# Pairwise attention scores with the sender term negated: minima in place of maxima, and the sign carried by the matmul's weights

## The chip, the cores and the metric

The kernel runs on one core of a Trainium2 chip. A core has four engines that this document speaks of: PE (TensorE, matrix multiply, fed by a weight load that the profile lists as PEld), DVE (VectorE, elementwise), ACT (ScalarE, activation functions) and POOL (GpSimd, elementwise). PE and the other engines meet through semaphores; PE writes to PSUM, the accumulator memory, and the rest lives in SBUF. The metric is the device time of one execution in microseconds (us), lower is better. Before the change it is 5019.07 us, the median of three runs that lie between 5017.83 and 5020.0 us.

## The reference

Input x holds 64 graphs of 256 nodes with 128 features; `adj` is one 256x256 matrix that all graphs share. Four layers follow one another, each of them x = x + layer(relu(layernorm(x))). Layers 1 to 3 are a sigmoid-gated aggregation, an attention with tanh and exp, and a gated recurrent unit with five steps. They are not touched by the change. Layer 0 is the costly one, and the change is all in it:

```python
s1 = jnp.einsum('bkf,ef->bke', x, W1)      # W = adj: W1 = adj[:, :128], W2 = adj[:, 128:]
s2 = jnp.einsum('bkf,ef->bke', x, W2)      # 256 features e
pre = s1[:, :, None, :] + s2[:, None, :, :] + b_lin
h = jnp.where(pre >= 0, pre, 0.2 * pre)
e = jnp.einsum('bije,e->bij', h, a) + bias
attn = jax.nn.softmax(e, axis=2)
out = jax.nn.sigmoid(jnp.einsum('bij,bjf->bif', attn, x))
```

For each graph, every ordered pair (i, j) of its 256 x 256 node pairs has 256 features that go through a leaky relu and are summed with the weights `a`. That is over a thousand million relus in all, and they are computed one by one.

## The kernel before, in words

**What is computed for a pair.** The leaky relu is split into a linear part and 0.8 times a relu. Of the linear part, what depends on i alone cancels in the softmax over j, and what depends on j comes from two matmuls (`v2_rep`, line 732). The features are reordered and scaled by |a| when the weights `w_p` are prepared (lines 219 to 304), so that a feature's weight is only +0.8 or -0.8; 256 features make two halves `ec` of 128, one feature on each partition. The relu tile of a node i is 128 features x 256 senders j, and there are 256 nodes x 2 halves of these for each of 64 graphs.

**Two ways to write a tile.** ACT computes relu(s2 + s1), with s1 as a bias that is one number per partition (line 698). DVE and POOL compute max(s2, -s1) instead, from a tile `s1n` that holds -s1 (DVE line 680, POOL line 703). The two differ by s1, which doesn't depend on j and so cancels in the softmax. `s2` is a copy in SBUF, DVE reads it in PSUM (`s2_ps`), and ACT after its first two half batches in a PSUM copy of its own (`s2_act`).

**Batches.** A batch is a tile `r` of eight node tiles (4 groups `g` of 32 nodes, times 2 places `k`), in a pool of 12 buffers (`BUFS`). It is made in two halves (`g2`), and either half can be made by DVE, ACT or POOL; DVE can make both at once. PE multiplies a batch by a window of `a_win` (lines 764 to 767): the window is 32 columns wide, zero but for one column with +-0.8, so the sum over 128 features lands in one row of the scores `e_ps`. Four matmuls with 32 columns each, one for each g, go side by side in the four column groups of PE. Each fp32 matmul shows as two instructions in the profile. A batch of `ec` 0 takes one matmul of 512 columns for each g, both k in one; a batch of `ec` 1 has different weights for its two k, and takes two matmuls of 256 columns for each g.

**Merges.** Two node rows take four batches: for each row one with `ec` 0 and one with `ec` 1. When at least `SPARE` = 5 finished batches wait for PE, two rows are made as three batches instead (`begin`, lines 609 to 623): in the first two, DVE adds max(s2, -s1) of the second feature half onto the places k = 0 of the `ec` 0 batch (`merge`, line 722), four instructions a batch; the third batch (`two`) holds the second feature half of the nodes k = 1 of both rows. So a merged pair of rows costs PE one batch less, and DVE eight merge instructions in place of eight tiles made by anyone.

**The order is planned when the program is built.** `Model` (lines 38 to 52) keeps a clock for each engine, and the last loop of the kernel gives the next piece of work to the engine whose clock allows it first. Its prices are constants: 365 ns for an ACT tile, 454 for a POOL tile, 1131 and 2198 ns for a half and a whole batch on DVE, 392 for a merge, 858 for a batch on PE. Other work (the layers of earlier graphs, the preparation of later ones) comes from generators, the chains, whose steps are fitted in between; helpers `act`, `dve`, `mm` add each step's price. Each engine then runs its instructions in the planned order, whatever their real durations are.

**Preparation of a group.** Groups are one or two graphs (`GROUPS`: 34 groups, 30 of them with two). For the first, `first_head` (line 475) computes s1 and s2; for the 33 others `head` (line 506) does the layer norm, the transposition and s1, and `senders` (line 555) s2. Here ACT writes `s1` (line 523) and `s1n` (line 525) from the same PSUM tile, each twice a group: 66 instructions each, 60 of them 512 wide. In `first_head` DVE writes `s1n` (line 492) and ACT `s1` (line 500).

Of the kernel before, what the change touches and what calls it, by code (L numbers as in the profile page):

```python
# [12 lines left out]
P = 128  # L13
# [42 lines left out]
def kernel(ctx: ExitStack, tc: tile.TileContext, ins: dict, out: bass.AP):  # L56
# [102 lines left out]
    make_identity(nc, ident)  # L159
    neg_half = constant([P, 4], "neg_half")  # L160
    nc.gpsimd.memset(neg_half, -0.5)
    a_win = constant([P, 2, 63], "a_win")
    nc.vector.memset(a_win, 0.0)
    a_rep = lent([P, 2, P], "a_rep", "h_t")
    nc.vector.memset(a_rep, 0.2)
# [46 lines left out]
    v2_rep = constant([P, P], "v2_rep")  # L212
    w_p = constant([P, 2, N], "w_p")
    blin_p = constant([P, 2], "blin_p")
    blin_n = constant([P, 2], "blin_n")
    left2 = constant([P, P], "left2")
    left_b = constant([P, 1], "left_b")

    def constants0():
# [56 lines left out]
                )  # L276
        yield "dve"
        dve(2).tensor_copy(blin_p, b_ps)
        dve(2).tensor_scalar(blin_n, b_ps, -1.0, None, ALU.mult)
        for half in (1, 0):  # L280
            yield "act"
            act(N).copy(w_p[:, half, :], p[:, half, :])
        counts["w_p"] += 2
        yield "dve"
        for c in range(2):
# [13 lines left out]
        dve(P).tensor_copy(v2_rep, v2_ps)  # L299

        for c in range(2):
            w = a_win[:, c, 31:32]
            dve(1).tensor_scalar(w, p_two[:, c : c + 1], n_pos, None, ALU.is_lt)
            dve(1).tensor_scalar(w, w, 1.6, -0.8, ALU.mult, ALU.add)

# [167 lines left out]
    def first_head(xt, to, snd):  # L475

        G, _, W = sizes(xt)
        h = yield from ln_relu(ap, xt, "h0", "h0", at=LANDS)
        h_t = yield from transpose_blocks(ap, h, "h0t", psum_h)
        to.update(h=h, h_t=h_t)  # L480
        yield "pe", lambda: counts["w_p"] > 1
        s2_ps, s1_ps = psum_h([P, 2, N], "s2_ps"), psum_a([P, 2, W], "s1_ps")
        for half, p in ((1, s2_ps), (0, s1_ps)):
            for ec in range(2):
                mm(
                    p[:, ec, :], lhsT=w_p[:, half, bass.ts(ec, P)], rhs=flat(h_t),
                    start=True, stop=True,
                )
        yield "dve"
        s1n = ap.tile([P, 2, W], F32, tag="s1n", name="s1n")  # L490
        for ec in range(2):
            dve(W, 1).tensor_scalar(
                s1n[:, ec, :], s1_ps[:, ec, :], -1.0, blin_n[:, ec : ec + 1], ALU.mult, ALU.add
            )
        yield "act"
        s2 = ap.tile([P, 2, N], F32, tag="s2", name="s2")
        act(2 * N).copy(s2, s2_ps)
        s1 = ap.tile([P, 2, W], F32, tag="s1", name="s1")
        for ec in range(2):
            act(W, 1, more=27).activation(  # L500
                s1[:, ec, :], s1_ps[:, ec, :], AF.Identity, bias=blin_p[:, ec : ec + 1]
            )
        to.update(s1=s1, s1n=s1n)
        snd.update(s2=s2, s2_ps=s2_ps)

    def head(xt, to):
        G, _, W = sizes(xt)
        h = yield from ln_relu(ap, xt, "h0", "h0")
        h_t = yield from transpose_blocks(ap, h, "h0t", psum_h, settled)
        to.update(h=h, h_t=h_t)  # L510
        if counts["left"] > 0:
            yield from bounds(to)
        for ec in range(2):
            yield "pe", lambda: counts["w_p"] > 0
            p = psum_h([P, W], "s1_ps")
            mm(
                p, lhsT=w_p[:, 0, bass.ts(ec, P)], rhs=flat(h_t), start=True, stop=True
            )
            yield "act", lambda: counts["w_p"] > 1
            if ec == 0:  # L520
                s1 = ap.tile([P, 2, W], F32, tag="s1", name="s1")
                s1n = ap.tile([P, 2, W], F32, tag="s1n", name="s1n")
            act(W, 1, more=27).activation(s1[:, ec, :], p, AF.Identity, bias=blin_p[:, ec : ec + 1])
            yield "act"
            act(W, 1, more=27).activation(
                s1n[:, ec, :], p, AF.Identity, bias=blin_n[:, ec : ec + 1], scale=-1.0
            )
        to.update(s1=s1, s1n=s1n)

    def bounds(of):  # L530

# [48 lines left out]
    class Pairs:  # L580
# [5 lines left out]
        def __init__(self, g, b, of, snd):  # L586
            self.g, self.b, self.of, self.snd = g, b, of, snd
            self.row = 0
            self.todo = []
            self.merges = []  # L590
            self.batches = []
            self.opened = False
            self.owned, self.by_act = {}, 0

            self.s1n_v = of["s1n"][:, :, bass.ts(b, N)].rearrange(
                "p c (k g t) -> p c g k t", k=2, g=4
            )
            self.s1n_b = of["s1n"][:, :, bass.ts(b, N)].rearrange(
                "p c (k g t) -> p c k g t", k=2, g=4
            )  # L600

# [7 lines left out]
        def begin(self):  # L609
            waiting = sum(x["halves"] == 2 for x in self.batches)  # L610
            merged = waiting >= SPARE and self.row < 31
            t = self.row

            if merged:
                kinds = ((t, 0, True, False), (t + 1, 0, True, False), (t, 1, False, True))
            else:
                kinds = ((t, 0, False, False), (t, 1, False, False))
            for t, ec, on_top, two in kinds:
                batch = {
                    "t": t, "ec": ec, "merged": on_top, "two": two, "halves": 0, "ready": 0.0  # L620
                }
                self.todo += [(batch, ec, 0), (batch, ec, 1)]
            self.row += 2 if merged else 1
# [35 lines left out]
        def make(self, who):  # L659
# [6 lines left out]
                self.batches.append(batch)  # L666
            r, t = batch["r"], batch["t"]
            s2 = self.snd["s2"] if who == "pool" else self.own(who)
            s1, s1n = self.of["s1"], self.of["s1n"]
            if who == "dve":  # L670
                whole = g2 == 0 and self.todo and self.todo[0][0] is batch
                if whole:
                    self.todo.pop(0)
                n = 4 if whole else 2
                if batch["two"]:
                    s1n = self.s1n_b[:, ec, 1, 2 * g2 : 2 * g2 + n, t : t + 2].unsqueeze(3)
                else:
                    s1n = self.s1n_v[:, ec, 2 * g2 : 2 * g2 + n, :, t : t + 1]
                model.op("dve", model.WHOLE if whole else model.HALF)
                nc.vector.tensor_tensor(  # L680
                    r[:, 2 * g2 : 2 * g2 + n, :, :],
                    s2[:, ec : ec + 1, :].unsqueeze(1).to_broadcast([P, n, 2, N]),
                    s1n.to_broadcast([P, n, 2, N]),
                    ALU.max,
                )
                if whole:
                    if batch["merged"]:
                        self.merges.append((model.t[who] + LAG[who], batch, 0))
                        g2 = 1
                    else:  # L690
                        self.whole(batch, who)
            else:
                for g, ic, i in self.nodes(batch, g2):
                    if g > 2 * g2 or ic:
                        yield
                    if who == "act":
                        model.op("act", model.TILE["act"] + 42 * (s2 is self.snd["s2"]))
                        nc.scalar.activation(  # L698
                            r[:, g, ic, :], s2[:, ec, :], AF.Relu, bias=s1[:, ec, i : i + 1]
                        )  # L700
                    else:
                        model.op("pool", model.TILE["pool"])
                        nc.gpsimd.tensor_scalar(  # L703
                            r[:, g, ic, :], s2[:, ec, :], FLT_MAX, s1n[:, ec, i : i + 1],
                            ALU.min, ALU.max,
                        )
            if batch["merged"]:
                self.merges.append((model.t[who] + LAG[who], batch, g2))
# [3 lines left out]
        def merge(self):  # L712

            _, batch, g2 = self.merges.pop(0)
            r = batch["r"]
            for g, ic, i in self.nodes(batch, g2):
                if ic:
                    continue
                if g > 2 * g2:
                    yield  # L720
                model.op("dve", model.MERGE)
                nc.vector.scalar_tensor_tensor(  # L722
                    r[:, g, ic, :], self.own("dve")[:, 1, :], self.of["s1n"][:, 1, i : i + 1],
                    r[:, g, ic, :], ALU.max, ALU.add,
                )
            self.whole(batch, "dve")

# [15 lines left out]
        def multiply(self):  # L743
# [10 lines left out]
                parts = ((1, t, 1, 0), (1, t + 1, 1, 1))  # L754
            elif batch["ec"]:
                parts = ((0, t, 0, 0), (1, t, 1, 1))
            else:
                parts = ((slice(0, 2), t, 0, slice(0, 2)),)
            for ic, t, sign, k in parts:
                for g in range(4):  # L760
                    to, of = self.e_ps[bass.ts(g, 32), ic, :], r[:, g, k, :]
                    if len(parts) == 1:
                        to, of = to.rearrange("p a b -> p (a b)"), flat(of)
                    nc.tensor.matmul(  # L764
                        to, lhsT=a_win[:, sign, 31 - t : 63 - t], rhs=of,
                        start=False, stop=self.over, skip_group_check=True,
                    )

# [543 lines left out]
```

## Time and profile before

| what | value |
|---|---|
| three runs, median (range) | 5019.07 us (5017.83 to 5020.0) |
| the profiled execution: span from first to last instruction | 5017.8 us |
| busy share PE / DVE / ACT / POOL | 99% / 98% / 98% / 95% |
| weight loads (PEld) | 46% |
| DMA, mean of the span | 6 GB/s |
| mean granted TensorE clock | 0.999 |

The profiled execution's own time is its span, 5017.8 us, some 1.3 us under the median of the runs. The page lists groups of instructions by line, engine and operation, with the names of the tiles that are written and read, the number of instructions, the busy time of the group in us, the mean duration of one in ns, and then the engine's idle time before them and what ended it. Instructions of ACT, DVE and PE overlap their neighbours at the ends: the mean duration of an ACT tile, 871 ns, is the time through the pipeline, and the distance from one start to the next is what a further instruction costs. The timeline gives such starts. The chain of waits follows the work that ended last back from the end, so a piece's duration there is the time it held up what came after it.

### The profile page before, as it was taken

The numbers are of one execution on the slowest core, as the hardware profiler recorded it, in microseconds if no ns is written. First come the engines' busy times: TensorE is split into PE (matmuls) and PEld (weight loads), VectorE is DVE, ScalarE is ACT, GpSimd is POOL, SyncE is SP. The second block draws the span as 40 slices with busy tenths as digits, with TensorE's granted clock in tenths as the row PEclk, the third lists the DMA queues.
The fourth block names the chain that finished last, engine by engine and source line by source line (L and its number), as shares of the span: only waits on it lengthen the run. The fifth ranks groups of instructions, "written<-read, shape, count | busy, mean of one in ns | idle before, by whom it ended". The sixth has DMA issues, their size and how long they took to land.

```text
span 5017.8 us, 176085 instructions
## 1 busy us (share of the span) xinstructions
PE 4985.7 (99%) x69627; PEld 2291.3 (46%) x69627; DVE 4895.7 (98%) x8591; ACT 4922.9 (98%) x12912; POOL 4778.0 (95%) x10637
## 2 busy tenths in 40 slices
PE   9999999999999999999999999999999999999998
PEld 4444444444444444444444444444444444444444
DVE  9999999999999999999999999999999999999994
ACT  8999999999999999999999999999999999999994
POOL 8999999999999999999999999999999999999881
PEclk9999999999999999999999999999999999999999
DMA  0000000000000000000000000000000000000000
GB/s 22 4 6 2 5 6 7 6 2 6 7 6 7 2 6 6 7 6 2 6 8 4 7 4 6 6 7 4 4 6 6 7 7 2 5 5 4 4 4 8
DMA packets 56109, 29.56 MB, mean 6 GB/s; under 512 B 20336, under 2 KB 55280, under 8 KB 55280
## 3 DMA queue, kind: packets, MB, share of 16 engines
q1 hardware_dynamic: 54736, 18.04, 1.5%
q8 instruction: 546, 8.95, 0.7%
q14 instruction: 283, 2.32, 0.2%
q10 hardware_dynamic: 544, 0.26, 0.0%
HBM read 9.84 MB, written 8.45 MB: 4 GB/s over the span
## 4 chain that ended last, share of the span: by engine, by line
PE 92%; DVE 4%; ACT 3%; issue 1%; POOL 0%; DMA 0%; DVEq 0%; ACTq 0%; POOLq 0%
PE e_ps L764 56%; PE gate_ps L109 8%; PE hv_ps L109 6%; PE m_ps L109 5%; PE s_ps L109 3%; DVE r L680 3%; PE o_ps L109 2%; PE e_ps L109 2%; ACT r L698 2%; PE rc_ps L109 2%; PE hn_ps L116 1%; PE rsum_ps L109 1%; PE e_ps L116 1%; PE h_t_ps L116 1%; DVE r L722 1%
## 5 line engine op out<-in xcount | busy, mean ns | idle before, releaser
L703 POOL TENSOR_SCALAR r<-s,s1n 128x256 f32<-128x256 f32 x10012 | 4528.5, 476 | 79.4 <-PE e_ps L764 36.4
L698 ACT ACTIVATE r<-s_act,s 128x256 f32<-128x256 f32 x9664 | 4170.7, 871 | 7.6 <-PE e_ps L764 6.0
L764 PE MATMUL e_ps<-r,a_win 128*32 128x256 f32 (+1 forms) x40144 | 3258.1, 467 | 3.4 <-DVE r L680 3.3
L680 DVE TENSOR_TENSOR r<-s_ps,s1n 128x1024 f32<-128x1024 f32 (+1 forms) x1281 | 2291.0, 1824 | 3.9 <-PE e_ps L764 3.9
L764 PEld LDWEIGHTS e_ps<-r,a_win 128*32 128x32 f32 x40144 | 1279.9, 110 | 1574.3 <-issue 853.6
L722 DVE SCALAR_TENSOR_TENSOR r<-s_ps,s1n,r 128x256 f32<-128x256 f32 x4504 | 1852.6, 471 | 1.7 <-POOL r L703 1.0
L698 ACT ACTIVATE r<-s,s 128x256 f32<-128x256 f32 x512 | 298.2, 1006 | 0.1
L109 PE MATMUL m_ps<-adj_t,hn 128*32 128x256 f32 x4096 | 248.0, 381 | 1.6 <-ACT hn L1089 1.6
L455 ACT ACTIVATE h<-x,bsh,brs 128x128 f32<-128x128 f32 x384 | 229.6, 850 | 5.6 <-POOL bsh L449 4.7
L109 PEld LDWEIGHTS m_ps<-adj_t,hn 128*32 128x32 f32 x4096 | 133.0, 110 | 118.2 <-issue 32.2
L1066 ACT ACTIVATE gate_ps<-gate_ps,bz 128x512 f32<-128x512 f32 (+1 forms) x170 | 170.8, 1005 | 2.7 <-PE gate_ps L109 2.7
L1068 ACT ACTIVATE hv_ps<-hv_ps,bh 128x512 f32<-128x512 f32 (+1 forms) x170 | 166.4, 979 | 6.5 <-PE hv_ps L109 6.5
L1038 ACT COPY m_t<-m_ps 128x512 f32<-128x512 f32 (+1 forms) x170 | 161.4, 949 | 9.3 <-PE m_ps L109 9.3
L1048 ACT ACTIVATE m_ps<-gate_ps,br 128x512 f32<-128x512 f32 (+1 forms) x170 | 161.0, 949 | 8.9 <-PE gate_ps L109 7.2
L109 PE MATMUL hv_ps<-rh,u_th 128*32 128x512 f32 (+1 forms) x1360 | 168.4, 567 | 0.9 <-DVE rh L1051 0.9
L109 PE MATMUL gate_ps<-m_t,t_w_w 128*32 128x512 f32 (+1 forms) x1360 | 168.1, 568 | 0.3 <-ACT m_t L1038 0.2
L109 PE MATMUL hv_ps<-m_t,t_w_w 128*32 128x512 f32 (+1 forms) x1360 | 168.5, 567 | 0.0
L109 PE MATMUL gate_ps<-m_t,w_t 128*32 128x512 f32 (+1 forms) x1360 | 168.4, 568 | 0.0
L1089 ACT COPY hn<-hn_ps 128x512 f32<-128x512 f32 (+1 forms) x136 | 126.5, 930 | 18.2 <-PE hn_ps L116 18.0
L109 PE MATMUL gate_ps<-hf,u_t 128*32 128x512 f32 (+1 forms) x1088 | 135.4, 567 | 0.0
L109 PE MATMUL s_ps<-h0t,w_p 128*32 128x256 f32 (+1 forms) x1568 | 134.9, 445 | 0.5 <-ACT h0t L471 0.5
L447 POOL TENSOR_TENSOR brs<-bve,neg_half 128x4 f32<-128x4 f32 (+1 forms) x136 | 133.5, 982 | 0.0
(213 smaller groups left out, 4388.1 us busy)
## 6 DMA issues: line engine op xcount, KB each, us to landing
xt<-in_x_dram SPq DMA_DIRECT2D x30, 256.0 KB
out_dram<-y SPq DMA_DIRECT2D x30, 256.0 KB
row<-rows SPq DMA_DIRECT2D x128, 0.5 KB
xt<-in_x_dram SPq DMA_DIRECT2D x4, 128.0 KB
out_dram<-y SPq DMA_DIRECT2D x4, 128.0 KB
bound<-row SPq DMA_DIRECT2D x30, 2.0 KB
raw_L_gnn_w_w<-in_L_gnn_w_w_dram SPq DMA_DIRECT2D x3, 128.0 KB
adj_n<-in_adj_dram ACTq DMA_DIRECT2D x1, 256.0 KB
```

The costliest lines, as they stand in the source:

```text
L109: nc.tensor.matmul(out[bass.ts(c, 32), :], lhsT=lhsT[:, bass.ts(c, 32)], rhs=rhs, **flags)
L116: nc.tensor.transpose(out, src, ident)
L455: act(P, 2, 1).activation(h[:, g, :], xt[:, g, :], AF.Relu, bias=shift[:, g : g + 1], scale=rstd[:, g : g + 1],)
L680: nc.vector.tensor_tensor(r[:, 2 * g2 : 2 * g2 + n, :, :], s2[:, ec : ec + 1, :].unsqueeze(1).to_broadcast([P, n, 2, N]), s1n.to_broadcast ...
L698: nc.scalar.activation(r[:, g, ic, :], s2[:, ec, :], AF.Relu, bias=s1[:, ec, i : i + 1])
L703: nc.gpsimd.tensor_scalar(r[:, g, ic, :], s2[:, ec, :], FLT_MAX, s1n[:, ec, i : i + 1], ALU.min, ALU.max,)
L722: nc.vector.scalar_tensor_tensor(r[:, g, ic, :], self.own("dve")[:, 1, :], self.of["s1n"][:, 1, i : i + 1], r[:, g, ic, :], ALU.max, ALU.add,)
L764: nc.tensor.matmul(to, lhsT=a_win[:, sign, 31 - t : 63 - t], rhs=of, start=False, stop=self.over, skip_group_check=True,)
L1038: act(W).copy(m_t, m_ps)
L1048: act(W, 1).activation(t_r, g_ps, AF.Tanh, bias=br, scale=0.5)
L1066: act(W, 1).activation(t_z, g_ps, AF.Tanh, bias=bz, scale=0.5)
L1068: act(W, 1).activation(cand, hv_ps, AF.Tanh, bias=bh)
```

## The change

`w_p`'s second half gets a factor -1, so s2 comes out negated (s2n). DVE and POOL then compute min(s2n, s1), which is -max(s2, -s1), and ACT computes relu(-s2n + s1) as before by giving its instruction the scale -1. So a half batch made by ACT is positive, one made by DVE or POOL negative. `a_win` gets a second copy with the opposite sign, and each half batch carries a mark (`up`, 1 for ACT) that selects the copy. The tile `s1n` is no longer made, nor is `blin_n`; in `first_head` DVE now writes `s1`, and ACT's two instructions there go. A merge keeps the place k = 0 negative: it subtracts an ACT half from the minimum, and adds any other. In a merged `ec` 0 batch with at least one ACT half, k = 0 is then negative and k = 1 positive, so its matmul of 512 columns for each g becomes two of 256 columns with their own weights. The planner's constants and its price of a batch stay as they are.

```diff
-    a_win = constant([P, 2, 63], "a_win")
+    a_win = constant([P, 2, 2, 63], "a_win")
...
-        dve(2).tensor_scalar(blin_n, b_ps, -1.0, None, ALU.mult)
         for half in (1, 0):
             yield "act"
-            act(N).copy(w_p[:, half, :], p[:, half, :])
+            act(N).activation(
+                w_p[:, half, :], p[:, half, :], AF.Copy, scale=-1.0 if half else 1.0
+            )
...
-            w = a_win[:, c, 31:32]
+            w, w_n = (a_win[:, up, c, 31:32] for up in (1, 0))
             dve(1).tensor_scalar(w, p_two[:, c : c + 1], n_pos, None, ALU.is_lt)
             dve(1).tensor_scalar(w, w, 1.6, -0.8, ALU.mult, ALU.add)
+            dve(1).tensor_scalar(w_n, w, -1.0, None, ALU.mult)
@@ -487,20 +488,15 @@
             dve(W, 1).tensor_scalar(
-                s1n[:, ec, :], s1_ps[:, ec, :], -1.0, blin_n[:, ec : ec + 1], ALU.mult, ALU.add
+                s1[:, ec, :], s1_ps[:, ec, :], blin_p[:, ec : ec + 1], None, ALU.add
             )
...
-        s1 = ap.tile([P, 2, W], F32, tag="s1", name="s1")
-        for ec in range(2):
-            act(W, 1, more=27).activation(
-                s1[:, ec, :], s1_ps[:, ec, :], AF.Identity, bias=blin_p[:, ec : ec + 1]
-            )
@@ -519,13 +515,8 @@
             act(W, 1, more=27).activation(s1[:, ec, :], p, AF.Identity, bias=blin_p[:, ec : ec + 1])
-            yield "act"
-            act(W, 1, more=27).activation(
-                s1n[:, ec, :], p, AF.Identity, bias=blin_n[:, ec : ec + 1], scale=-1.0
-            )
@@ -666,22 +658,22 @@
                 nc.vector.tensor_tensor(
                     r[:, 2 * g2 : 2 * g2 + n, :, :],
                     s2[:, ec : ec + 1, :].unsqueeze(1).to_broadcast([P, n, 2, N]),
-                    s1n.to_broadcast([P, n, 2, N]),
-                    ALU.max,
+                    s1.to_broadcast([P, n, 2, N]),
+                    ALU.min,
                 )
...
+                batch["up"][g2] = int(who == "act")
...
                         nc.scalar.activation(
-                            r[:, g, ic, :], s2[:, ec, :], AF.Relu, bias=s1[:, ec, i : i + 1]
+                            r[:, g, ic, :], s2[:, ec, :], AF.Relu, bias=s1[:, ec, i : i + 1],
+                            scale=-1.0,
                         )
...
                         nc.gpsimd.tensor_scalar(
-                            r[:, g, ic, :], s2[:, ec, :], FLT_MAX, s1n[:, ec, i : i + 1],
-                            ALU.min, ALU.max,
+                            r[:, g, ic, :], s2[:, ec, :], FLT_MAX, s1[:, ec, i : i + 1],
+                            ALU.min, ALU.min,
                         )
@@ -720,8 +714,8 @@
                 nc.vector.scalar_tensor_tensor(
-                    r[:, g, ic, :], self.own("dve")[:, 1, :], self.of["s1n"][:, 1, i : i + 1],
-                    r[:, g, ic, :], ALU.max, ALU.add,
+                    r[:, g, ic, :], self.own("dve")[:, 1, :], self.of["s1"][:, 1, i : i + 1],
+                    r[:, g, ic, :], ALU.min, ALU.subtract if up else ALU.add,
                 )
@@ -754,15 +748,18 @@
             elif batch["ec"]:
                 parts = ((0, t, 0, 0), (1, t, 1, 1))
+            elif batch["merged"] and any(batch["up"]):
+                parts = ((0, t, 0, 0), (1, t, 0, 1))
             else:
                 parts = ((slice(0, 2), t, 0, slice(0, 2)),)
             for ic, t, sign, k in parts:
                 for g in range(4):
                     to, of = self.e_ps[bass.ts(g, 32), ic, :], r[:, g, k, :]
+                    up = 0 if batch["merged"] and k == 0 else batch["up"][g // 2]
                     if len(parts) == 1:
                         to, of = to.rearrange("p a b -> p (a b)"), flat(of)
                     nc.tensor.matmul(
-                        to, lhsT=a_win[:, sign, 31 - t : 63 - t], rhs=of,
+                        to, lhsT=a_win[:, up, sign, 31 - t : 63 - t], rhs=of,
                         start=False, stop=self.over, skip_group_check=True,
                     )
```

## The prediction

> **What bounds the kernel now.** I read the page's busy times first; they leave the question open, because all four engines are nearly full. The table by stretches, taken over the body of the run without its first 60 and last 138 us, sharpens it, and PE's waits in the same stretch decide it (who waited for whom: us, times, longest).
>
> ```profile
> PE 4985.7 (99%) x69627; PEld 2291.3 (46%) x69627; DVE 4895.7 (98%) x8591; ACT 4922.9 (98%) x12912; POOL 4778.0 (95%) x10637
> ```
> ```profile
> 60.00:4880.00 4820.00, 4816.00 (x67235) 2211.84 (x67236) 4777.39 (x8355) 4803.91 (x12615) 4699.93 (x10448) 1.00 0.02 5
> ```
> ```profile
> PE left_ps L109 <- DVE r L680: 1.2, 2, 0.8
> PE e_ps L764 <- DVE r L680: 1.1, 2, 0.8
> ```
>
> In 4820 us PE stands idle for 4, and its longest visible wait is 0.8 us. Idle in the same order are DVE 43, ACT 16 and POOL 120 us. So PE binds at every moment, and the makers of tiles (DVE, ACT, POOL) are within a few per cent of it: the planner has traded PE's batches against DVE's merges until both are full. The time falls only if PE gets fewer or cheaper batches. The groups that carry layer 0, and pieces of the chain of waits (start, us held, what):
>
> ```profile
> L703 POOL TENSOR_SCALAR r<-s,s1n 128x256 f32<-128x256 f32 x10012 | 4528.5, 476 | 79.4 <-PE e_ps L764 36.4 <-DVE v_rep L299 9.5 <-issue 7.6
> L698 ACT ACTIVATE r<-s_act,s 128x256 f32<-128x256 f32 x9664 | 4170.7, 871 | 7.6 <-PE e_ps L764 6.0 <-POOL bmm L445 1.2
> L764 PE MATMUL e_ps<-r,a_win 128*32 128x512 f32 x16384 | 2038.8, 593 | 2.6 <-DVE r L680 2.6
> L722 DVE SCALAR_TENSOR_TENSOR r<-s_ps,s1n,r 128x256 f32<-128x256 f32 x4504 | 1852.6, 471 | 1.7 <-POOL r L703 1.0 <-ACT r L698 0.5
> L764 PE MATMUL e_ps<-r,a_win 128*32 128x256 f32 x23760 | 1527.9, 380 | 0.8 <-DVE r L680 0.7
> ...
> L698 ACT ACTIVATE r<-s,s 128x256 f32<-128x256 f32 x512 | 298.2, 1006 | 0.1
> ```
> ```profile
> 2499.61 0.86 PE e_ps L764 x8
> 2500.46 0.86 PE e_ps L109 x16
> ...
> 2518.71 0.87 PE e_ps L109 x32
> ...
> 2520.44 1.72 PE hv_ps L109 x16
> ...
> 2538.40 1.73 PE m_ps L109 x32
> ```
>
> Counting: 4504 merges at eight a pair are 563 merged pairs of rows. 64 graphs x 32 rows are 2048 rows; two batches each, less one a merged pair, are 3533 batches. The matmuls agree: 2048 batches of `ec` 0 with 8 instructions of 512 columns are 16384, and 2048 - 563 = 1485 others with 16 of 256 are 23760. A batch holds PE for 0.86 us in either form.
>
> **What the change removes.** ACT's 66 instructions of line 525. Their price is the distance between starts, not their span:
>
> ```profile
> 1976.24 1.09 ACT L523 ACTIVATE s<-s_ps,blin_p 128x512 f32<-128x512 f32 x1
> 1976.81 0.88 ACT L698 ACTIVATE r<-s_act,s 128x256 f32<-128x256 f32 x1
> 1977.17 1.11 ACT L525 ACTIVATE s1n<-s_ps,blin_n 128x512 f32<-128x512 f32 x1
> 1977.74 1.27 ACT L698 ACTIVATE r<-s_act,s 128x256 f32<-128x256 f32 x2
> ```
>
> A 512-wide one takes 0.57 us, a 256-wide tile 0.36: 60 x 0.57 + 6 x 0.36 = 36 us of ACT. The planner prices 0.578 and 0.365, so 36.9, and 0.7 for the two instructions of `first_head`: 37.6 us. Nobody on PE's path waits for them, so their own removal gives PE nothing; it pays through the planner. 37.6 us are 103 ACT tiles. The makers' rate is 1/0.365 + 1/0.454 + 8/2.198 = 8.58 tiles a us. One more merged pair saves PE 0.858 us, saves the makers 8 tiles and costs DVE 8 x 0.392 = 3.14 us, which is 11.4 of its tiles: net 3.4 tiles. If the plan shortens by d us, it has d/0.858 pairs more, and the makers lose 8.58 d tiles: 103 = 8.58 d + 3.4 d/0.858, so d = 8.2 us, with 9.6 more pairs. The ends: 0, if ACT's freed time only turns into waiting for buffers (POOL's row shows 36.4 us of waits for PE to free one); and 30 pairs or 26 us, if the makers lose nothing by a shorter run because their true idle time (16 to 120 us above) covers it. I take 8, because the planner sees its own prices and both sides full, and keep 0 and 26 for the range.
>
> **What it adds on PE.** Merged `ec` 0 batches with an ACT half go from 8 instructions of 512 columns to 16 of 256. There are 2 x 563 = 1126 merged ones. ACT makes 9664 + 512 of 28264 tiles, 36%; a batch has two halves, so 36% to 59% of them contain one of ACT, 405 to 665: I take 535. By the chain, 32 instructions of 256 hold PE for 1.73 us and 16 of 512 for 1.72, so a split costs 5 ns (0 to 10 by the rounding): 535 x 5 = 3 us, ends 0 and 11 us if all 1126 cost 10. The 128-column piece, 0.87 us for four times as many instructions, shows the same: no visible fixed part. The planner does not price this, and PE has no idle time to cover it, so all of it is added. Twice the weight loads lie under matmuls, as they already do in the 1485 batches of 256 columns; PEld is busy 46%.
>
> The Trainium skill, "TensorEngine Tiling (Array Packing)", section Instruction Overhead, speaks against the split: each matmul has an overhead of about 60 cycles. At the 2.4 GHz of its page "Trainium Kernel Development and Optimization" (section NeuronCore Architecture) that is an estimated 25 ns for each of two more rounds of four matmuls, so 535 x 50 ns = 27 us and a run of 5038 us. The rows above say 5 ns a batch, and I go by them.
>
> **What it moves, at no cost.** DVE's max becomes min, and its add sometimes subtract: among 128x512 tensor_tensors a subtract (line 1072) has a mean of 677 ns, a multiplication (line 974) 678; 1 in 678 of DVE's 4144 us on lines 680 and 722 is 6 us either way, under its 43 idle. ACT's scale -1: line 525 has it, line 523 has not, and both step by 0.57 us, so 0; the reading leaves 10 ns either way, 102 us over ACT's 10176 tiles, against a cover of 16 us idle, so this end is kept with the POOL rival below. POOL's second operation max becomes min, and no row of before shows that pair. The nearest row is line 703 itself, same form and width; the lowest end is the same operation on 4 columns (0.19 us, against 0.45 a tile: 0.26 less), the highest a power on 4 columns, 0.83 us more than the 0.19:
>
> ```profile
> 2401.30 18.98 POOL L703 TENSOR_SCALAR r<-s,s1n 128x256 f32<-128x256 f32 x42
> 2420.37 0.19 POOL L444 TENSOR_SCALAR bve<-bmv 128x4 f32<-128x4 f32 x1
> ...
> 2420.80 1.02 POOL L447 TENSOR_TENSOR brs<-bve,neg_half 128x4 f32<-128x4 f32 x1
> ```
>
> Both ends are far off; I take 0. A cheaper POOL tile would gain little, because the order is fixed and PE is the bound. At the start, `first_head` loses two ACT instructions (0.84 us) but DVE gets two more tiny ones for `a_win` (0.15 each) ahead of its first batch: within half a us, taken as 0. No wait is added: readers of `s1` wait for ACT as those of `s1n` did, and no DMA or queue is touched.
>
> **The new order** is a term of its own. PE's chain has pieces of 0.99 where 0.86 would do, and weight loads wait for a maker some 650 times in the body (389 for POOL, 125 for ACT, 95 and 45 for DVE); at 0.13 us each that is an estimated 85 us, and a tenth more or less is 8 us. In the last 118 us PE is idle 18; a third of that, 6, may move. I take 0 for both, and 8 to 10 us as the spread around each case.
>
> **Sum.** 5017.8 - 8.2 + 2.7 = 5012.3 for the span; with the 1.3 us by which the median stands above it, 5014 us.
>
> **The rivals.**
> - *The gain goes nowhere* (ACT idles or waits for buffers, merges stay near 4504): 5019 + 3 = 5022 us. For it: POOL's and ACT's waits for PE's buffers. Against: the planner merges whenever five batches wait, so any surplus turns into merges.
> - *More merges than the balance*: 26 us less, 3 more, 4996 us. For it: idle time of DVE and POOL; against: the planner doesn't see that idle time.
> - *POOL's min with min is slower than min with max*, the one that ends on the slower side. Place: line 703, 9867 tiles in the body. The planner would go on giving POOL as many tiles. It decides from 120 us / 9867 = 12 ns a tile (3%) on; beyond that each ns costs 9.9 us, so at 25 ns 5014 + 128 = 5142 us. For it: POOL's operations do differ (power 1.02 against 0.19). Against: the same form, one comparison for another.
> - *The split costs more than 5 ns*, by weight loads that no longer hide: at two uncovered loads of 110 ns a batch, 535 x 0.22 = 118 us, 5129. Against: the 1485 batches that are split already hold PE 0.86 us.
>
> The Trainium skill, "GPSIMD Engine Reference", section 3.1, says that loops of at most two operations an element are bound by ports at 1.03 cycles an element; that would make all pairs equal, at an estimated 0.22 us for 256 columns at 1.2 GHz. The trace has 0.45, so that bound is not what sets this tile, and the page can't close the POOL rival.
>
> **How the numbers follow.** A measurement tells 0.2%, 10 us, from no change: faster is under 5009, slower over 5029. Likeliest 0.62, with its own range 5004 to 5024 (about a fifth under 5009); gain nowhere 0.18; more merges 0.12; slow POOL (or ACT) 0.05; dear split 0.03. Faster: 0.62 x 0.22 + 0.12 = 0.26; slower: 0.08 and some 0.02 of the tails, 0.10; the rest, 0.64, within 0.2%. The range for 8 in 10 leaves out the two dear cases and about half of the many-merges case: 4998 to 5030.
>
> **What would show it.** Right: line 525 gone, line 523 still 66; merges (line 722) up from 4504 to about 4580, ACT tiles up by some 80, POOL's down by some 20; the 512-column group of line 764 down by 8 for each split batch, about 4300, the 256-column group up by about 8400; PE still without waits. The split is dear if the sixteens of line 764 hold over 0.87 us each in the chain; the POOL rival shows as a step over 0.46 us. Wrong would make me, above all, a plan whose merges go down, or a tail laid out differently.

## The result and the profile after

The changed kernel takes 11592.83 us, the median of six runs, against 5019.97 us for the kernel before beside it: 2.309 times as long, with a 95% interval from 2.307 to 2.312. I had forecast 5014 us within 4998 to 5030. The term that failed is POOL's, which I had put at 0.

The page of the changed kernel: span, busy times, granted clock by slices, the shares of the chain that ended last, and the groups of layer 0 (line 697 is POOL's tile, 761 PE's batch, 716 the merge, 691 ACT's tile).

```profile
span 11591.5 us, 188542 instructions
...
PE 7343.1 (63%) x75947; PEld 2890.9 (25%) x75947; DVE 5056.6 (44%) x8674; ACT 5020.1 (43%) x12924; POOL 11435.9 (99%) x10629
...
PEclk9988787788887878878877777878878888778878
...
POOL 56%; issue 11%; PE 4%; DVE 1%; ACT 0%; POOLq 0%; DVEq 0%; ACTq 0%
...
L697 POOL TENSOR_SCALAR r<-s,s 128x256 f32<-128x256 f32 x10004 | 11184.5, 1139 | 30.2 <-DVE s L493 9.1
L761 PE MATMUL e_ps<-r,a_win 128*32 128x256 f32 (+1 forms) x46464 | 5331.8, 496 | 2482.6 <-POOL r L697 2366.0
L716 DVE SCALAR_TENSOR_TENSOR r<-s_ps,s,r 128x256 f32<-128x256 f32 x4600 | 2016.3, 479 | 4665.4 <-POOL r L697 4553.8
L691 ACT ACTIVATE r<-s_act,s 128x256 f32<-128x256 f32 x9744 | 3797.7, 538 | 466.1 <-PE e_ps L761 444.8
```

Before, four engines were full. Now POOL is full, PE is 63% busy and DVE and ACT under 45%. POOL's group has 10004 tiles where it had 10012, but a mean of 1139 ns where it had 476. Most of the others' idle time goes back to POOL: DVE's merges waited 4554 us for POOL's tiles and PE's batches 2366. The timeline of POOL gives the distance from start to start (start, us, engine, what, count):

```profile
2499.11 17.89 POOL L697 TENSOR_SCALAR r<-s,s 128x256 f32<-128x256 f32 x16
2517.08 0.20 POOL L445 TENSOR_SCALAR bve<-bmv 128x4 f32<-128x4 f32 x1
```

16 tiles in 17.89 us are 1.12 us a tile, against 0.45 before (42 in 18.98; the medians of the distances are 1.117 and 0.451). The difference times 10004 is 6.7 ms more on POOL, and the run is 6.57 ms longer. POOL's small multiply-add on 4 columns costs what it cost before.

### The profile page after: what moved, and what is told of

Same layout as the page of the kernel before. It is cut to its first block, busy times and chain, and to the rows that moved or that the text cites. A ratio compares the mean times of both kernels' runs of the same rounds, so it can differ in the third digit from the quotient of the medians.

```text
span 11591.5 us, 188542 instructions
## 1 busy us (share of the span) xinstructions
PE 7343.1 (63%) x75947; PEld 2890.9 (25%) x75947; DVE 5056.6 (44%) x8674; ACT 5020.1 (43%) x12924; POOL 11435.9 (99%) x10629
## 4 chain that ended last, share of the span: by engine, by line
POOL 56%; issue 11%; PE 4%; DVE 1%; ACT 0%; POOLq 0%; DVEq 0%; ACTq 0%
POOL r L697 55%; PE e_ps L761 2%; POOL brs L448 1%; PE gate_ps L109 1%; DVE r L672 0%; PE hv_ps L109 0%; PE m_ps L109 0%; DVE r L716 0%; ACT r L691 0%; POOL x1b L883 0%; POOL bsh L450 0%; POOL bmm L446 0%; POOL bve L445 0%; PE s_ps L109 0%; PE o_ps L109 0%
## 5 line engine op out<-in xcount | busy, mean ns | idle before, releaser
L697 POOL TENSOR_SCALAR r<-s,s 128x256 f32<-128x256 f32 x10004 | 11184.5, 1139 | 30.2 <-DVE s L493 9.1
L761 PE MATMUL e_ps<-r,a_win 128*32 128x256 f32 (+1 forms) x46464 | 5331.8, 496 | 2482.6 <-POOL r L697 2366.0
L716 DVE SCALAR_TENSOR_TENSOR r<-s_ps,s,r 128x256 f32<-128x256 f32 x4600 | 2016.3, 479 | 4665.4 <-POOL r L697 4553.8
L691 ACT ACTIVATE r<-s_act,s 128x256 f32<-128x256 f32 x9744 | 3797.7, 538 | 466.1 <-PE e_ps L761 444.8
L761 PEld LDWEIGHTS e_ps<-r,a_win 128*32 128x32 f32 x46464 | 1760.4, 122 | 5575.1 <-POOL r L697 4005.5
L672 DVE TENSOR_TENSOR r<-s_ps,s 128x2048 f32<-128x2048 f32 (+1 forms) x1267 | 2252.6, 1813 | 124.9 <-PE e_ps L761 122.7
L109 PE MATMUL m_ps<-adj_t,hn 128*32 128x256 f32 x4096 | 325.0, 405 | 2.7 <-ACT hn L1086 2.5
L109 PE MATMUL gate_ps<-m_t,w_t 128*32 128x512 f32 (+1 forms) x1360 | 264.8, 679 | 0.0
L116 PE MATMUL h_t_ps<-ident,h 128*128 128x128 f32 x256 | 82.8, 393 | 275.3 <-ACT h L456 274.1
L116 PE MATMUL hn_ps<-ident,hf 128*128 128x128 f32 x512 | 104.8, 335 | 142.2 <-DVE hf L1075 139.5
```

The source lines that it names most:

```text
L109: nc.tensor.matmul(out[bass.ts(c, 32), :], lhsT=lhsT[:, bass.ts(c, 32)], rhs=rhs, **flags)
L116: nc.tensor.transpose(out, src, ident)
L672: nc.vector.tensor_tensor(r[:, 2 * g2 : 2 * g2 + n, :, :], s2[:, ec : ec + 1, :].unsqueeze(1).to_broadcast([P, n, 2, N]), s1.to_broadcast( ...
L691: nc.scalar.activation(r[:, g, ic, :], s2[:, ec, :], AF.Relu, bias=s1[:, ec, i : i + 1], scale=-1.0,)
L697: nc.gpsimd.tensor_scalar(r[:, g, ic, :], s2[:, ec, :], FLT_MAX, s1[:, ec, i : i + 1], ALU.min, ALU.min,)
L716: nc.vector.scalar_tensor_tensor(r[:, g, ic, :], self.own("dve")[:, 1, :], self.of["s1"][:, 1, i : i + 1], r[:, g, ic, :], ALU.min, ALU.su ...
```

## The experiments

Two theories could explain a slow POOL. **A**: the pair of operations min with min is itself slow there. **B**: the pair is not to blame, but something around it is (the operand `s1`, its buffer, the sharing of SBUF with the other engines). Each ratio below compares a run with runs of the kernel before on the same chip.

**The pairs by themselves.** A small kernel that leaves out the computation and has 24 POOL instructions for each pair. In the trace they take turns in twos: one min with max, one min with min, and so on. For example:

```diff
+    for _ in range(24):
+        nc.gpsimd.tensor_scalar(min_max[:, 0:256], s[:, 0:256], FLT_MAX, c[:, 0:1], ALU.min, ALU.max)
+    for _ in range(24):
+        nc.gpsimd.tensor_scalar(min_min[:, 0:256], s[:, 0:256], FLT_MAX, c[:, 0:1], ALU.min, ALU.min)
```

> A small kernel that leaves out the whole computation and writes zeros: 12 or 24 POOL instructions in a row for each pair of operations, on 128x256 fp32 from one SBUF tile, three pairs also on DVE, and two pairs in four widths. Theory A (the pair itself is slow on POOL): min with max 0.45 us from start to start, min with min about 1.12 us; the slow pair's extra should grow with the width if it is per element. Theory B (the pair is not the cause; something around it in the changed kernel slows POOL: the operand s1, its buffer, or sharing SBUF with DVE): both pairs 0.45 us here. Both theories: DVE's pairs do not differ. Open for both: whether max with min, or a single min, is at the fast price.

The groups of that kernel, a line for each pair; the name of the tile says the pair, `ptr` that the first scalar is the pointer and the second the constant, `only` a single operation (count, then busy us and mean ns):

```profile
L95 POOL TENSOR_SCALAR min_min_wide<-s,c 128x1024 f32<-128x1024 f32 x12 | 44.3, 3694 | 0.0
L35 POOL TENSOR_SCALAR min_min<-s,c 128x256 f32<-128x256 f32 x24 | 27.7, 1155 | 0.0
L50 POOL TENSOR_SCALAR mult_min<-s,c 128x256 f32<-128x256 f32 x24 | 27.4, 1144 | 0.1
...
L41 POOL TENSOR_SCALAR max_max<-s,c 128x256 f32<-128x256 f32 x24 | 27.3, 1139 | 0.0
...
L47 POOL TENSOR_SCALAR add_max<-s,c 128x256 f32<-128x256 f32 x24 | 27.3, 1137 | 0.0
...
L38 POOL TENSOR_SCALAR max_min<-s,c 128x256 f32<-128x256 f32 x24 | 27.2, 1133 | 0.0
...
L62 POOL TENSOR_SCALAR only_min<-s,c 128x256 f32<-128x256 f32 x24 | 22.1, 923 | 0.0
L86 POOL TENSOR_SCALAR min_max_wide<-s,c 128x1024 f32<-128x1024 f32 x12 | 13.4, 1114 | 0.0
L32 POOL TENSOR_SCALAR min_max<-s,c 128x256 f32<-128x256 f32 x24 | 11.6, 482 | 4.4 <-DMA c<-in_adj_dram 4.4
L56 POOL TENSOR_SCALAR mult_add<-s,c 128x256 f32<-128x256 f32 x24 | 11.5, 478 | 2.2
L68 POOL TENSOR_SCALAR ptr_min_max<-s,c 128x256 f32<-128x256 f32 x24 | 11.4, 474 | 0.0
...
L89 POOL TENSOR_SCALAR min_min_four<-s,c 128x4 f32<-128x4 f32 x12 | 3.7, 309 | 0.0
L80 POOL TENSOR_SCALAR min_max_four<-s,c 128x4 f32<-128x4 f32 x12 | 3.2, 268 | 0.0
```

Theory A holds, in a sharper form than I had it. Of the 14 two-operation variants tried (11 pairs, three of them also with their scalars exchanged), min with max and mult with add last 474 to 482 ns, min with max in both orders of its scalars. All the others last 1133 to 1155, max with min among them, and a single operation 923, almost twice a fast pair. For mult with add this holds of the duration alone: it ran in turn with min with add, and some 0.09 us of idle time stood between the two, so that from its start to the next one's 0.57 us passed, where min with max took 0.45. Why is open.

```profile
205.22 0.48 POOL L56 TENSOR_SCALAR mult_add<-s,c 128x256 f32<-128x256 f32 x1
205.79 1.15 POOL L59 TENSOR_SCALAR min_add<-s,c 128x256 f32<-128x256 f32 x1
```

From 256 to 1024 columns min with max grows by (1114 - 482) / 768 = 0.82 ns a column, min with min by (3694 - 1155) / 768 = 3.3. On 4 columns they are only 41 ns apart. On DVE I had expected no difference; the three pairs tried have means of 410 to 508 ns, min with min between the others, so none is slow as on POOL.

The Trainium skill, "GPSIMD Engine Reference", section 3.1, gives 1.03 cycles an element for loops of at most two operations, an estimated 0.86 ns at the 1.2 GHz of "Trainium Kernel Development and Optimization" (section NeuronCore Architecture). The slope of min with max, 0.82, agrees with it; that of min with min, also two operations, is four times as steep, so the number of operations does not tell the price.

**The pair exchanged in the kernel before, and a second slow pair in the changed one.**

```diff
-                            r[:, g, ic, :], s2[:, ec, :], FLT_MAX, s1n[:, ec, i : i + 1],
-                            ALU.min, ALU.max,
+                            r[:, g, ic, :], s2[:, ec, :], -FLT_MAX, s1n[:, ec, i : i + 1],
+                            ALU.max, ALU.max,
```

> The kernel before with one edit: POOL computes max(s2, -FLT_MAX) and then the max with s1n, in place of min with FLT_MAX and then max; same values, same planned order. Theory A, if two equal operations are slow: 10012 tiles at 1.12 us on POOL, so some 11400 to 11700 us. Theory B: 5020 us, no change.

11574 us, one run, with the old operands, the old order and everything else of the kernel before. Theory B is out: the pair alone makes a loss of 6555 us (11574.3 - 5019.4), where the changed kernel lost 6573. Its group by shape:

```profile
L703 POOL TENSOR_SCALAR r<-s,s1n 128x256 f32<-128x256 f32 x10012 | 11168.8, 1135 | 27.6 <-DVE v_rep L299 9.8 <-PE e_ps L764 4.1 <-issue 0.2
```

```diff
-                            r[:, g, ic, :], s2[:, ec, :], FLT_MAX, s1[:, ec, i : i + 1],
-                            ALU.min, ALU.min,
+                            r[:, g, ic, :], s2[:, ec, :], -FLT_MAX, s1[:, ec, i : i + 1],
+                            ALU.max, ALU.min,
```

> The changed kernel with one edit: POOL computes max(s2n, -FLT_MAX) and then the min with s1, in place of min with FLT_MAX and then min; same values. Theory A, if max with min is a fast pair as min with max is: POOL tiles back at 0.45 us, and the rest of the prediction holds, about 5014 us (5004 to 5024). Theory A, if any pair but min with max is slow: about 11600 us. Theory B: about 11600 us, since operands and buffers stay as in the changed kernel.

11568.1 us (ratio 2.305, 2.302 to 2.308): max with min is as slow, as it is in the small kernel. My guess that its mirror image shares the fast price was wrong.

**The change with a fast pair.** The same value can be had as a min with `s1` and then a max with -FLT_MAX, which changes nothing:

```diff
-                            r[:, g, ic, :], s2[:, ec, :], FLT_MAX, s1[:, ec, i : i + 1],
-                            ALU.min, ALU.min,
+                            r[:, g, ic, :], s2[:, ec, :], s1[:, ec, i : i + 1], -FLT_MAX,
+                            ALU.min, ALU.max,
```

> The changed kernel with POOL's two operations the other way about: first the min with s1, then a max with -FLT_MAX, so the pair is min with max; same values, same planned order. Theory A (the pair, and nothing else, made the kernel slow): POOL tiles at 0.45 us and the other terms of the prediction as they stand, with the 814 split batches counted in the changed kernel at the 3 ns each that splitting alone has measured (3.0 us for 1126): 5017.8 - 8.2 + 2.4 and 1.3, 5013 us (5004 to 5024). Theory B, that something else in the change slows POOL or the rest: far above 5030 us.

5017.07 us, against 5021.94 for the kernel before: ratio 0.9990, 0.9982 to 0.9999. So the rest of the change is worth 4.9 us, a tenth of a per cent, and the interval only just excludes zero gain. It is the fastest version of this study. Its page, and the groups by shape:

```profile
span 5012.7 us, 188542 instructions
...
PE 4978.0 (99%) x75947; PEld 2494.4 (50%) x75947; DVE 4890.7 (98%) x8674; ACT 4915.8 (98%) x12924; POOL 4742.0 (95%) x10629
```
```profile
L697 POOL TENSOR_SCALAR r<-s,s 128x256 f32<-128x256 f32 x10004 | 4492.8, 477 | 92.9 <-PE e_ps L761 51.7 <-DVE s L493 9.7 <-ACT r L691 4.7
...
L761 PE MATMUL e_ps<-r,a_win 128*32 128x256 f32 x36592 | 2240.0, 380 | 3.8 <-DVE r L672 3.6
L716 DVE SCALAR_TENSOR_TENSOR r<-s_ps,s,r 128x256 f32<-128x256 f32 x4600 | 1889.3, 471 | 2.3 <-POOL r L697 2.1
...
L761 PE MATMUL e_ps<-r,a_win 128*32 128x512 f32 x9872 | 1269.7, 593 | 2.5 <-DVE r L672 2.5
```

The planned order is that of the changed kernel (the counts are equal); only the pair differs. Merges are 4600, 12 pairs more than before, which is 12 x 0.858 = 10.3 us less for PE. The 512-column group has fallen by 16384 - 9872 = 6512, or 814 split batches of 8 instructions.

**The split by itself**, in the kernel before, for all its 1126 merged batches of the first half:

```diff
             elif batch["ec"]:
                 parts = ((0, t, 0, 0), (1, t, 1, 1))
+            elif batch["merged"]:
+                parts = ((0, t, 0, 0), (1, t, 0, 1))
```

> The kernel before with every merged batch of the first feature half (1126 of them) multiplied by two matmuls of 256 columns for each g in place of one of 512, and nothing else changed. My term (5 ns a batch by the chain, 0 to 10): 5026 us (5020 to 5031). Rival (a fixed cost for each matmul, or weight loads that no longer hide, 50 to 220 ns a batch): 5076 to 5270 us.

5022.44 against 5019.43 us, ratio 1.0008 (1.0000 to 1.0017): 3.0 us, or 3 ns a batch, with an interval up to 8. A fixed cost for each matmul, 50 ns a batch, would have been 56 us, and uncovered weight loads more. The estimate that the prediction worked out from "TensorEngine Tiling (Array Packing)", section Instruction Overhead, by adding some 60 cycles for each further matmul, does not hold for this stream.

**ACT's work put back.** The 66 instructions for the negated s1 return in the fast version, writing a tile that nobody reads:

```diff
+                s1n = ap.tile([P, 2, W], F32, tag="s1n", name="s1n")
             act(W, 1, more=27).activation(s1[:, ec, :], p, AF.Identity, bias=blin_p[:, ec : ec + 1])
+            yield "act"
+            act(W, 1, more=27).activation(
+                s1n[:, ec, :], p, AF.Identity, bias=blin_p[:, ec : ec + 1], scale=-1.0
+            )
```

> The same kernel, with the 66 ACT instructions that made the negated s1 put back in head; they write a tile that nobody reads, and the planner prices them. If the gain comes from the removed ACT work by way of the planner's balance: the merges fall back from 4600 to about 4505 and the time rises by 8 us against the run without them, to some 5021 us. If the gain comes from elsewhere (a shorter chain of steps, a different tail): no rise, or one that does not go with the number of merges.

5024.99 us (5022.8 to 5027.35) against 5017.07 (5014.86 to 5020.86): the runs don't overlap, and the 7.9 us are the 8 forecast. Merges are 4472, 16 pairs fewer (I had expected about 4505), and PE's busy time rises from 4978.0 to 4990.2 us, near the 13.7 that 16 batches cost. So the gain comes from ACT's freed time, and it reaches PE as fewer batches. That it stands in proportion to the merges is argued from two plans only, and no run frees ACT's time while it holds the merges still. In the fast pair POOL's tile steps by 448 ns where it stepped by 451, but both runs have that pair, so it is not where the gain comes from.

**The planner told.** The slow pair as in the changed kernel, with its real price in the plan:

```diff
-    TILE = {"act": 365, "pool": 454}
+    TILE = {"act": 365, "pool": 1120}
```

> The changed kernel with its slow pair, and the planner told of it: the price of a POOL tile is 1120 in place of 454 ns. If the slow pair costs only its share of the makers' rate once it is planned for: POOL makes 0.89 in place of 2.20 tiles a us, 6300 tiles fewer in 4820 us; giving up all 573 merged pairs makes up 1950 tiles and lets PE run 492 us longer, in which the makers make 3580 at 7.27 tiles a us, and the rest takes 108 us more: about 5610 us (5550 to 5750). If the time were bound by the price of the pair whatever the order: near 11600 us.

5637 us, one run. POOL now makes 4652 tiles, ACT 12028 where it made 10256, and merges are 1480 (185 pairs; I had worked with none). The group lines:

```profile
L697 POOL TENSOR_SCALAR r<-s,s 128x256 f32<-128x256 f32 x4652 | 5202.8, 1161 | 22.9 <-DVE s L493 9.4
L691 ACT ACTIVATE r<-s_act,s 128x256 f32<-128x256 f32 x11516 | 5171.5, 1371 | 0.0
```

So of the 6573 us lost, about 615 (5637 - 5022, its own kernel before) are what the slow pair costs in an order planned with its price, and 5956 (11593 - 5637) are the price of a fixed order that was planned with 454 ns.

**Where a late POOL begins to cost.** The kernel before, with every eighth, and in another run every 24th, POOL tile made by two instructions of half the width; the planner is not told:

```diff
+                        counts["tiles"] = counts.get("tiles", 0) + 1
+                        step = N // 2 if counts["tiles"] % 8 == 0 else N
+                        for j in range(0, N, step):
...
```

> The kernel before with every eighth POOL tile made by two instructions of 128 columns in place of one of 256, and the planner not told. By the small kernel's steps (0.240 us for 4 columns, 0.451 for 256, so 0.343 for 128) that is 0.235 us more for 1251 tiles, 294 us of POOL or 29 ns a tile. By the POOL rival's working (120 us idle are the cover, then each ns a tile costs 9.9 us): 5019 + 174 = 5193 us. If the cover were nothing: 5313. If POOL had far more room than its idle time shows: near 5020.

> The kernel before with every 24th POOL tile made by two instructions of 128 columns: 417 x 0.239 = 100 us more for POOL, 10 ns a tile. The POOL rival as first worked out (a cover of 120 us, so nothing happens under 12 ns a tile): 5020 us. The cover as the run with every eighth tile showed it (299 us more for POOL, 251 more in time, so 48 us): about 5072 us.

5273 and 5072 us, one run each. A tile in two halves takes 239 ns more (twice 345 less 451, from start to start). Of 299 us more on POOL, 251 came through (5273.4 - 5021.9), and of 100, 51 (5071.6 - 5020.2): covers of 48 and 49 us. The 120 us that the table of stretches leaves POOL without work are not the cover. With every eighth tile halved, POOL's waits in the same stretch from 60 to 4880 us are down to 0.3 us (us, times, longest), and still 42 of the 4820 us are not busy (the last of the five busy times is POOL's):

```profile
POOL r L706 <- ACT r L698: 0.3, 1, 0.3
```
```profile
60.00:4880.00 4820.00, 4706.62 (x63821) 2171.40 (x63822) 4575.00 (x7858) 4586.44 (x12007) 4777.52 (x11138) 1.00 0.02 5
```

So about 42 of the 120 us were no room that a slower POOL could use. The other 78 are POOL's waits in the kernel before; the longest of them:

```profile
POOL r L703 <- PE e_ps L764: 36.4, 26, 4.5
POOL bve L444 <- DVE bmv L439: 21.6, 33, 1.8
POOL r L703 <- issue: 7.6, 4, 2.4
```

Why 48 of these 78 us covered a late POOL, and not all, is not shown.

**A plan with more merges.** Prices of a batch of 868 and 878 ns in the fast version, and 868 in the kernel before, each with the one edit:

```diff
-    BATCH = 858
+    BATCH = 868
```

> The changed kernel with the fast pair, and the planner's price of a batch on PE raised from 858 to 868 ns, so that it merges more. PE never waits in the real run while POOL waits some 50 us for it. By the balance: 8.58 x (35 - 0.868 m) = 3.41 m, m = 28 more merged pairs, 224 more merges, and 24 us less for PE. If the makers' real room covers it: 4993 us. If it does not (the plan of the makers is 11 us longer): 5010 to 5028.

> The kernel before with the same price of 868 ns. By the same balance 224 more merges than 4504 and 24 us less, 4998 us, if the makers keep up. The change's own gain (5 us between the two kernels at 858) should stand between this run and the one with the fast pair at 868.

> The same at a price of 878 ns: twice the extra merges (some 55 pairs), 47 us less for PE. The makers' plan would be 22 us longer than at 858, within the 48 us of cover that POOL showed but above the 16 us for which ACT is idle: I expect this to be slower than at 868, above 4993 us, with PE waiting for ACT or DVE for the first time.

The ratios, in this order, are 1.0002 (0.9992 to 1.0011), 1.0016 (1.0006 to 1.0025) and 1.0015 (1.0005 to 1.0024), where the fast version had 0.9990 at 858. Merges rose to 4784, 4704 and 4936, that is by 184, 200 and 336 where I had worked out 224, 224 and some 440. So PE had fewer batches, yet none became faster; the forecasts of 4993 and 4998 us failed with their condition, that the makers keep up. The tables by stretches show part of where it went, for the fast version at 868 and then at 878 (stretch, its length, busy PE, PEld, DVE, ACT, POOL):

```profile
60.00:4880.00 4820.00, 4803.57 (x73360) 2404.36 (x73360) 4782.24 (x8598) 4803.97 (x12638) 4671.73 (x10454) 1.00 0.02 6
```
```profile
60.00:4880.00 4820.00, 4787.85 (x73142) 2394.41 (x73144) 4783.24 (x8700) 4801.47 (x12631) 4674.94 (x10460) 1.00 0.02 6
```

DVE and ACT stand near where they stood (4777 and 4804 us before), and PE idles for 16 and 32 us, where it was 4 in the kernel before and 6 in the fast version. I read this as makers without room to give. Over the whole span, 23 and 42 fewer batches than in the fast version should have taken 20 and 36 us from PE; its busy time fell by 5.6 and 14.9 and its idle time rose by 10.5 and 26.0. What lengthened the rest of its busy time is not shown. Between the two kernels at 868 the change still gains 0.14%, as it does 0.10% at 858.

## Why the prediction was wrong

**The step that failed** is the one on POOL in the part on moved work: "The nearest row is line 703 itself, same form and width; ... I take 0." The pair costs 1.117 us, 666 ns more than the 451 I carried over. I had both hints in hand and misread them. The power row showed that POOL's price depends on the operation, but I called it far off and let the same form decide. And the rows that I took for the lower end, mult with add on 4 columns, could not have shown the difference: it is 41 ns at that width, and mult with add is itself one of the two pairs of short duration. The prediction also held the tile's 0.45 us against an estimate of 0.22 for 256 columns; by the small kernel a tile of 4 columns already takes 0.24 from start to start, and only the rest grows with the width. That estimate, too, would have made all pairs equal.

**The POOL rival had the mechanism, the place and the direction**, and a chance of 0.05 with an example of 25 ns, where the size was 666. Its working, an order that doesn't know and then 9.9 us for each ns, gives 5014 + (666 - 12) x 9.9 = 11489 for the true size, 0.9% under the run. Its point of decision was mis-sized: the cover is 48 us (5 ns a tile), not 120 (12 ns), because I read as room all the time that busy spans leave free.

**PE as the bound, and the balance through merges**: right, as far as the fast version shows. ACT's 36 us (line 525) became 12 more merged pairs where 9.6 were worked out; merges 4600 (I said 4580), ACT's tiles 10256, up 80 (I said 80), POOL's down 8 (I said 20).

**The split**: the price was right (5 ns, 0 to 10; measured 3, 0 to 8), the number was not. 814 of 1150 merged batches contain an ACT half, 71%, above the 59% that I had as the upper end. Independent halves at ACT's average share of 36% were no upper bound. Either the halves of a batch go to different makers more often than by chance, or ACT makes more than its share of the merged batches; the runs don't tell which. At 3 ns the splits cost 2.4 us, so the term of 3 came out near the mark because a high count met a low price, which is luck.

**DVE's min and ACT's scale at no cost**: right. In the fast version the median distance from one start to the next stays 392 ns for a merge and 356 for an ACT tile, and a whole batch on DVE keeps its mean of 2276 ns.

**The sum without POOL**: 5014 against 5019, a gain of 5; measured 4.9. That the two agree so closely is partly luck: 12 pairs less the splits are 7.9 us, PE's busy time in one profile of each kernel does fall by 7.7 (4985.7 to 4978.0), but its idle time grows by 2.6, which the sum did not have. The rival "gain goes nowhere" is excluded by the run with ACT's work put back; "more merges" by the runs with another batch price; "the split costs more" by the split alone.

## What to carry to other kernels

An elementwise operation that is exchanged for its twin is a new instruction for POOL: where no row shows that very pair at that width, the range should reach to the engine's slowest row (here 0.83 us more a tile, where 0.67 were measured), and a small kernel that runs the candidates one after another prices them all at once. In an order that is planned from fixed prices, a wrong price costs far more than the slower instruction itself, here ten times as much. The time that busy spans leave free on an engine is not its room: of POOL's 120 us, 48 were.

## What I had not expected of the hardware

POOL's tensor_scalar on 128x256 fp32 has a mean of some 480 ns for min with max, with its scalars in either order, and for mult with add (which had gaps before it), of 1133 to 1155 ns for the eleven other two-operation variants that the small kernel held, and of 923 for one operation alone. Which of the untried pairs are fast stays open, and so does the reason.

The granted clock of PE was 0.812 over the changed kernel, where PE was busy for 63% of the time, and 0.998 in the version with the planner told, where it was 98%:

```profile
core 0: 11591.5 us, clock 0.812
```

The 512-column matmuls of layer 0 had a mean of 690 ns there against 593 before. It did not set the time, since POOL was late throughout. What it would cost a kernel in which such a PE is nearly the bound, no run here shows.
